# Diagonal loaded by quarters, layer 2's first mask in free tiles, bias of layer 2 behind the last norm

## The chip, the cores and the metric

The kernel runs on one core of one Trainium2 chip. The metric is device time in microseconds (us) of one execution; the median of three runs is given. The profile is of one further execution, recorded by the hardware profiler. The engines are PE (matrix products), DVE (vector), ACT (scalar), POOL (GpSimd) and SP, which here only issues transfers (DMAs). Each engine works through its own list of instructions in order.

## What is computed

`x` has the shape (8, 2048, 64): batch, nodes, channels. `adj` is a 2048 × 2048 matrix whose nonzero elements in a row are all the same number, 1/degree, and whose diagonal is nonzero. Four layers run one after the other, each adding its result to `x` and normalizing over the channels:

```python
x = _layernorm(x + L0(x, adj, embedding, weight, bias))   # weights made per node from an embedding
x = _layernorm(x + L1(x, H, adj, W, W_ind, ...))          # attention over 64 hyperedges, and adj @ (x @ W_ind)
x = _layernorm(x + L2(x, adj, weight_self, weight_neighbor, bias))
x = _layernorm(x + L3(x, adj, W))                         # adj + I, scaled by degree on both sides

# L0: the terms x, adj x and 2 adj (adj x) - x, each times a per-node weight
As = [jnp.eye(N)]; As.append(A)
for _ in range(2, K): As.append(2.0 * (A @ As[-1]) - As[-2])

# L2
out_self = jnp.einsum('bni,io->bno', x, weight_self)
x_neighbors = jnp.einsum('nm,bmi->bni', adj, x)
out_neighbors = jnp.einsum('bni,io->bno', x_neighbors, weight_neighbor)
return out_self + out_neighbors + bias
```

## The kernel before, in words

`x` is held as 2048 rows of 512 numbers (8 batches × 64 channels), in 16 tiles of 128 rows. A product with `adj` is made with a mask of zeros and ones, which is exact in the fast matmul format, and the row's number is multiplied in afterwards. That number is the diagonal of `adj`: the column buffer `s1` holds it, 128 partitions × 16, one column for each tile of rows; `s2` is twice that (L499). The other factor of a product is split in two parts of that format, `hi` and `lo`, and both are multiplied. A mask of 128 columns and 2048 rows is 1 MB.

The stages, in the order of the profile:

- **First product** (0 to 148 us), `first_product`: y1 = adj x. There are 4 quarters `q` of 4 row tiles, and in each 8 pieces `n` of adjacency (512 KB), with 16 matmuls of about 0.229 us each. The call `begin(n + 2)` ahead of piece n's products has SP load the piece and DVE turn it into a mask (L447), so DVE stands two pieces ahead. In quarter 0 each `begin` also loads a piece of `x` (512 KB, xraw) and splits it into x_hi (ACT, L425) and x_lo (DVE, L426); x and adjacency share a pool of four raw buffers. At the end of a quarter ACT and DVE write y_hi and y_lo of its tiles with the scale `s1`. Between the matmuls stand steps of `prepare`, which makes lists out of H for layer 1: small PE products (sm, L381 and L399), DVE operations (pT_raw, L366, and its neighbours) and some transfers.
- **Layer 0** (148 to 718 us), `layer0`: it loads adjacency again by row tile (adj, L958), x (xT, L969; xs, L973), the embedding (et, L971), and the row `s_row` spread to all partitions (srow, L964), all on SP. DVE makes masks (L978), and SP stores them in DRAM (L979) for the later layers. POOL and DVE compare mask × `s_row` with the adjacency itself, and so check that its rows have the form that the kernel uses. The first loads are issued while the first product still runs.
- **Layer 1** (718 to 1072 us), `layer1`: its order is written out by hand as a list of turns under `program_order`, which makes the scheduler keep the order of the source. The layer's norm is in steps: the variance on DVE, epsilon and the power −1/2 on POOL (L829, L831), the scale on ACT (x2, L835). When the turns reach the last tiles, `layer2_steps` is advanced beside them: `features2` transposes a tile of the new x, and `layer2(j)` multiplies it by layer 2's two weights (u, L858), writes y_hi on ACT and y_lo on DVE, adds the self term to x2 on DVE (L867) and the bias to x2 on POOL (L871). `for _ in last: pass` finishes the steps that are left after the turns.
- **Layer 2** (1072 to about 1210 us): for each of 16 row tiles, a mask is loaded (L1394), multiplied with y_hi and y_lo (32 matmuls, L1399), and DVE adds `s1` × product to x2 (L1508). `mask_tile` takes the mask's buffer from a pool of three, mj2, opened after layer 1; its space was that of layer 1's buffers, so the first load waits for layer 1's last readers.
- **Layer 3** (to the end).

Tiles of 256 KB named `b0_0` to `b0_15` make up a buffer that first holds x_hi. Later they are given to other uses one by one: layer 1 takes most of them for names of its own. `industry_early` loads layer 1's first mask in four parts into four of them.

The diagonal is loaded at piece n = 7 of the source, L451 to L461, by four DMAs that POOL issues, one for each quarter (2 KB: 128 × 4 single elements), and a fifth, also POOL's, writes `s1` to DRAM as the row `s_row` of 2048 numbers, one element at a time. Since nothing holds them back, they stand first on POOL's queue.

Of the kernel before, what the change touches and what calls it, by code (L numbers as in the profile page):

```python
# [18 lines left out]
P = 128  # L19
# [12 lines left out]
class Tiles:  # L32
# [6 lines left out]
    def __getitem__(self, key):  # L39
        p, t, c = key  # L40
        if self.per == 1:
            return self.tiles[t][p, c]
        k, lo = divmod(c.start, QW)
        return self.tiles[t * self.per + k][p, lo:lo + c.stop - c.start]


def r_(ap):
# [4 lines left out]
def kernel(  # L52
# [358 lines left out]
    def first_product(own, pre, rawp, mskp, y_hi, y_lo, prepare):  # L411

        x_hi, x_lo = buffer(own, 0, "x_hi"), buffer(own, 1, "x_lo")
        with tc.tile_pool(name="acc0", bufs=7, space=PSUM) as ps_acc, tc.tile_pool(
            name="sm0", bufs=1, space=PSUM
        ) as ps_s:
            def split_x(g, h):
                raw = rawp.tile([P, 2, QW], F32, tag="raw", name=f"xraw_{g}_{h}")
                lo = g * QW + h * 2 * P
                nc.sync.dma_start(  # L420
                    raw, xn[lo:lo + 2 * P, :].rearrange("(t p) c -> p t c", p=P)
                )
                for t in range(2):
                    j = 4 * g + 2 * h + t
                    nc.scalar.copy(r_(x_hi[:, j, :]), raw[:, t, :])  # L425
                    nc.vector.tensor_tensor(  # L426
                        r_(x_lo[:, j, :]), raw[:, t, :], x_hi[:, j, :], ALU.subtract
                    )

            steps = prepare(ps_s)  # L430
            pieces = [
                (q, i, kk, h)
                for q in range(NQ)
                for i, kk in enumerate([q] + [kk for kk in range(4) if kk != q])
                for h in range(2)
            ]
            m_of, accs = {}, {}

            def begin(n):

                if n >= len(pieces):
                    return
                q, i, kk, h = pieces[n]
                raw = rawp.tile([P, 2, QW], F32, tag="raw", name=f"raw_{q}_{kk}_{h}")
                nc.sync.dma_start(raw, at[q, kk][:, 2 * h:2 * h + 2, :])
                m = mskp.tile([P, 2, QW], F32, tag="m", name=f"m_{q}_{kk}_{h}")
                nc.vector.tensor_scalar(r_(m), raw, 0.0, None, op0=ALU.is_gt)  # L447
                m_of[n] = m
                if q == 0:
                    split_x(kk, h)  # L450
                if n == 7:  # L451

                    for qq in range(NQ):
                        d = at[qq, qq]
                        nc.gpsimd.dma_start(
                            cols_of["s1"][:, 4 * qq:4 * qq + 4],
                            bass.AP(d.tensor, d.offset, [[4 * QW + 1, P], [QW + P, 4]]),
                        )
                    nc.gpsimd.dma_start(
                        s_row.rearrange("o (t p) -> p (o t)", p=P), cols_of["s1"]  # L460
                    )  # L461

            with program_order():
                begin(0)
                begin(1)
                for n, (q, i, kk, h) in enumerate(pieces):
                    begin(n + 2)
                    if i + h == 0:
                        accs[q] = [
                            ps_acc.tile([P, BC], F32, tag="acc", name=f"y1p_{4 * q + jj}")  # L470
                            for jj in range(4)
                        ]
                    m = m_of.pop(n)
                    for t in range(2):
                        mt = 4 * kk + 2 * h + t
                        for jj in range(4):
                            for part in (x_hi, x_lo):
                                nc.tensor.matmul(  # L478
                                    accs[q][jj],
                                    r_(m[:, t, jj * P:(jj + 1) * P]),  # L480
                                    r_(part[:, mt, :]),
                                    start=i + h + t == 0 and part is x_hi,
                                    stop=i == 3 and h + t == 2 and part is x_lo,
                                )
                        if n > 8 or (n, t) == (6, 0):
                            for _ in range(1 + t):
                                next(steps, None)
                    if (i, h) == (3, 1):
                        for jj in range(4):
                            j = 4 * q + jj  # L490
                            s = cols_of["s1"][:, j:j + 1]
                            nc.scalar.activation(r_(y_hi[:, j, :]), accs[q][jj], AF.Copy, scale=s)
                            nc.vector.scalar_tensor_tensor(
                                r_(y_lo[:, j, :]), accs[q][jj], s, y_hi[:, j, :],
                                op0=ALU.mult, op1=ALU.subtract,
                            )
                for _ in steps:
                    pass
            nc.vector.tensor_scalar(cols_of["s2"], cols_of["s1"], 2.0, None, op0=ALU.mult)  # L499

    @with_exitstack
    def layer1(
# [345 lines left out]
        def layer2(j):  # L848

            xT = xT_of.pop(j)  # L850

            pool, tag = ((ps_g, "g"), (ps_fc, "fc"))[j % 2]
            mm = pool.tile([P, 2, BC], F32, tag=tag, name=f"u_{j}")
            mm = mm.rearrange("p h (r c) -> p h r c", r=NP)
            for pr in range(NP):
                for h in range(2):
                    rs = slice(h * 64, (h + 1) * 64)
                    nc.tensor.matmul(  # L858
                        mm[:, h, pr, :], xT[rs, pr * P:(pr + 1) * P], w2_sb[rs],
                        start=True, stop=True,  # L860
                    )

            def by_half(t):
                return t[:, j, :].rearrange("p (r h c) -> p h r c", h=2, c=C)

            nc.scalar.copy(r_(by_half(i_hi)), mm[:, :, :, 0:C])
            nc.vector.tensor_tensor(by_half(x2), mm[:, :, :, C:2 * C], by_half(x2), ALU.add)  # L867
            nc.vector.tensor_tensor(
                r_(by_half(i_lo)), mm[:, :, :, 0:C], by_half(i_hi), ALU.subtract
            )  # L870
            nc.gpsimd.tensor_tensor(  # L871
                b_view(x2[:, j, :]), b_view(x2[:, j, :]),
                bias2_sb.unsqueeze(1).to_broadcast([P, B, C]), ALU.add,
            )

# [35 lines left out]
        with program_order():  # L913
            run(unit, 0, first)
            run(unit, 0, second)
            run(unit, 1, first)
            for t in range(NT + 3):
                now = {"p": (product, t), "q": (product, t - 1), "u": (unit, t + 1), "v": (unit, t + 2),
                       "s": (unit, t), "m": (mixer, t - 1), "o": (mixer, t - 2),
                       "f": (mixer, t - 3)}  # L920
                for turn_ in turns.split():
                    who, what = turn_.split(".")
                    run(*now[who], what)
                    if t > NT and 0 <= now[who][1] < NT:
                        next(last, None)
            for _ in last:
                pass
        return x2


    def layer0(
# [288 lines left out]
        def industry_early():  # L1220


            parts = []
            for q, home in enumerate((4, 6, 13, 14)):
                m = own.tile([P, 4, P], F32, tag=f"b0_{home}", name=f"m0_{q}")
                nc.sync.dma_start(m, masks[0][:, 4 * q:4 * q + 4, :])
                parts.append(m)
            acc = ps_acc.tile([P, BC], F32, tag="acc", name="ind_0")

            def steps():  # L1230
                for mt in range(NT):
                    for part in (y_hi, y_lo):
                        nc.tensor.matmul(
                            acc, r_(parts[mt // 4][:, mt % 4, :]), r_(part[:, mt, :]),
                            start=mt == 0 and part is y_hi, stop=mt == NT - 1 and part is y_lo,
                        )
                    yield
# [101 lines left out]
    def short_program(top):  # L1339
# [71 lines left out]
        with tc.tile_pool(name="l0", bufs=1) as l0, tc.tile_pool(  # L1411
# [39 lines left out]
                nc.vector.tensor_scalar(flag, bad[:, 0:1], -1.0, 1.0, op0=ALU.mult, op1=ALU.add)  # L1451


        x2 = layer1(
            own, wts, fcw_sb, fcb_sb, av_sb, fcg_sb, vecs, rden, hgr, aggp, agg_st, h_sb, y_hi,
            y_lo, mask_tile, times_mask, w2_sb, bias2_sb, ps_acc, early,
        )
# [3 lines left out]
        with tc.tile_pool(name="mj2", bufs=3) as mjp, tc.tile_pool(  # L1461
# [38 lines left out]
                )  # L1500

            for j in range(NT):
                a = mask_tile(mjp, j, "l2")
                acc = ps_acc.tile([P, BC], F32, tag="acc", name=f"a2_{j}")
                for mt in range(NT):
                    times_mask(acc, a, y_hi, y_lo, mt)
# [624 lines left out]
```

## Time and profile before

| | |
|---|---|
| median of 3 runs | 1344.24 us (1344.21 to 1349.38) |
| the profiled execution | 1349.78 us, its span 1347.8 us |
| PE busy | 1275.1 us, 95% |
| DVE busy | 915.7 us, 68% |
| POOL busy | 483.8 us, 36% |
| ACT busy | 370.7 us, 28% |
| mean granted PE clock | 0.960 |

The profiled execution is 5.5 us above the median, and 2.0 us of it lie outside the span. Times of single instructions are of this execution. A line of a timeline gives the start in us, the length, the engine, the line of the source, the operation with output and input, the number of instructions, and in brackets how long the engine idled before and for whom. The chain of waits is followed back from the last instruction; its pieces are given in order of time.

The transfers concerned, from the table of DMA issues (name, queue, number, size of one, median us from issue to landing):

```profile
raw<-in_at SPq DMA_DIRECT2D x32, 512.0 KB, 5.5
xraw<-in_xn SPq DMA_DIRECT2D x8, 512.0 KB, 5.5
s<-in_at POOLq DMA_DIRECT2D x4, 2.0 KB, 6.3
s_row<-s POOLq DMA_DIRECT2D x1, 8.0 KB, 11.5
mj_l<-mask SPq DMA_DIRECT2D x47, 1024.0 KB, 4.9
```

POOL's queue at the start and around layer 1's last norm:

```profile
1.36 1.00 POOL L455 DMA_DIRECT2D s<-in_at  x1 [0.36 <-issue]
2.72 2.27 POOL L455 DMA_DIRECT2D s<-in_at  x3
...
1054.15 1.27 POOL L871 TENSOR_TENSOR x<-x,bias_sb 128x512 f32<-128x512 f32 x1 [0.21 <-DVE x L867]
1055.94 1.27 POOL L871 TENSOR_TENSOR x<-x,bias_sb 128x512 f32<-128x512 f32 x1 [0.52 <-DVE x L867]
1057.18 0.23 POOL L829 TENSOR_SCALAR var<-var 128x8 f32<-128x8 f32 x1
1057.50 1.67 POOL L831 TENSOR_TENSOR rstd<-var,mhalf 128x8 f32<-128x8 f32 x1
1059.13 1.26 POOL L871 TENSOR_TENSOR x<-x,bias_sb 128x512 f32<-128x512 f32 x1
```

The whole span in 40 slices of 33.7 us (PE's busy tenths and its granted clock):

```profile
PE   6999899999999999999997599999998799999997
PEclk9999899999999999999997599999998999999999
```

### The profile page before, as it was taken

Reading aid. Unit: us, or ns where it says so; the run is one execution under the profiler, and the core shown is the slowest. Engines: PE = TensorE matmul, PEld = TensorE weight load, DVE = VectorE, ACT = ScalarE, POOL = GpSimd, SP = SyncE. Lnnn points to the kernel's source line nnn. Section 1 sums busy time; section 2 is a strip of 40 time slices with the busy share of each in tenths; the row PEclk is TensorE's granted clock in tenths of the full one; section 3 lists DMA queues with packets and bytes.
Section 4 is the critical chain, followed back from the end, with each engine's and each line's share of the span. In section 5 each row is a group of like instructions: output and inputs, shape, how many; then the busy total and the mean of one; then the engine's idle time right before and its main releaser. Section 6 shows DMA issues by size and latency. Waiting matters only on the chain.

```text
span 1347.8 us, 19945 instructions
## 1 busy us (share of the span) xinstructions
PE 1275.1 (95%) x7708; PEld 1010.0 (75%) x7708; DVE 915.7 (68%) x1559; ACT 370.7 (28%) x853; POOL 483.8 (36%) x403
## 2 busy tenths in 40 slices
PE   6999899999999999999997599999998799999997
PEld 5777688888888888888885376666666588888885
DVE  3556378787877777777663669899984646655454
ACT  2100101111222222222212446666664511111111
POOL 2000354444444444444210667777772600000000
PEclk9999899999999999999997599999998999999999
DMA  8976632333333333331604022222220133333451
GB/s 219 269 215 182 197 112 89 104 105 104 105 104 105 105 105 105 105 105 55 256 23 152 24 75 77 91 95 94 79 78 1 49 140 125 125 120 139 171 188 72
DMA packets 100358, 157.21 MB, mean 117 GB/s; under 512 B 12832, under 2 KB 64416, under 8 KB 94112
## 3 DMA queue, kind: packets, MB, share of 16 engines
q1 hardware_dynamic: 97776, 151.65, 34.7%
q10 hardware_dynamic: 2304, 4.20, 0.8%
q8 instruction: 63, 1.03, 0.3%
q14 instruction: 39, 0.32, 0.1%
q0 software_dynamic: 176, 0.02, 0.1%
HBM read 118.08 MB, written 37.76 MB: 116 GB/s over the span
## 4 chain that ended last, share of the span: by engine, by line
PE 77%; DVE 14%; DMA 3%; ACT 2%; issue 1%; POOL 1%; SPq 0%; DVEq 0%; ACTq 0%; POOLq 0%
PE pp L1081 25%; PE a L1399 18%; PE y2p L1044 9%; PE y1p L478 7%; PE ind L1399 4%; DVE d L703 3%; PE df L802 2%; DMA xraw<-in_xn 2%; DVE gp L700 2%; DVE gate L654 2%; DVE ez L723 1%; PE try L154 1%; PE yp L1489 1%; DVE coef L658 1%; DVE th L798 1%
## 5 line engine op out<-in xcount | busy, mean ns | idle before, releaser
L1092 DVE SCALAR_TENSOR_TENSOR r<-pp,emb_sb,r 128x256 f32<-128x256 f32 x512 | 247.2, 483 | 114.9 <-PE pp L1081 101.1
L1081 PE MATMUL pp<-w_sb,xT 64*128 64x256 f32 x1024 | 160.4, 390 | 1.7 <-DVE r L1092 1.7
L1030 POOL TENSOR_TENSOR r<-xs,bn 128x256 f32<-128x256 f32 x32 | 22.7, 731 | 384.8 <-issue 245.3
L1081 PE MATMUL pp<-w_sb,y1T 64*128 64x256 f32 x1024 | 153.5, 376 | 0.0
L1081 PE MATMUL pp<-w_sb,y2T 64*128 64x256 f32 x1024 | 153.5, 376 | 0.0
L478 PE MATMUL y1p<-x_hi,m 128*128 128x512 f32 x256 | 105.9, 414 | 12.0 <-ACT x_hi L425 11.6
L1081 PEld LDWEIGHTS pp<-w_sb,xT 64*128 64x128 f32 x1024 | 94.4, 186 | 25.1 <-issue 14.9
L1081 PEld LDWEIGHTS pp<-w_sb,y1T 64*128 64x128 f32 x1024 | 99.7, 187 | 10.9
L1081 PEld LDWEIGHTS pp<-w_sb,y2T 64*128 64x128 f32 x1024 | 99.6, 187 | 11.0
L1399 PE MATMUL a<-y_hi,mj_l 128*128 128x512 f32 x256 | 102.9, 402 | 5.0 <-DMA mj_l<-mask 5.0
L1399 PE MATMUL ind<-y_hi,mj_l 128*128 128x512 f32 x240 | 104.8, 437 | 0.0
L1044 PE MATMUL y2p<-y_hi,msk 128*128 128x512 f32 x256 | 103.4, 404 | 0.0
L1399 PE MATMUL a<-y_lo,mj_l 128*128 128x512 f32 x256 | 102.7, 401 | 0.0
L478 PE MATMUL y1p<-x_lo,m 128*128 128x512 f32 x256 | 102.6, 401 | 0.0
L1044 PE MATMUL y2p<-y_lo,msk 128*128 128x512 f32 x256 | 101.5, 396 | 0.0
L1399 PE MATMUL a<-v_hi,mj_l 128*128 128x512 f32 x256 | 100.1, 392 | 0.0
L1399 PE MATMUL a<-v_lo,mj_l 128*128 128x512 f32 x256 | 100.0, 391 | 0.0
L1399 PE MATMUL ind<-y_lo,mj_l 128*128 128x512 f32 x240 | 96.7, 403 | 0.0
L725 POOL TENSOR_TENSOR ez<-ez,coef 128x1024 f32<-128x1024 f32 x32 | 69.9, 2184 | 71.3 <-DVE ez L723 69.0
L986 POOL TENSOR_TENSOR ms<-msk,srow 128x1024 f32<-128x1024 f32 x32 | 89.9, 2810 | 5.2 <-DVE ms L999 5.2
L478 PEld LDWEIGHTS y1p<-x_hi,m 128*128 128x128 f32 x256 | 49.3, 192 | 24.8 <-ACT x_hi L425 12.0
L978 DVE TENSOR_SCALAR msk<-adj 128x1024 fp32r<-128x1024 f32 x32 | 63.7, 2024 | 3.9 <-DMA adj<-in_at 3.8
(273 smaller groups left out, 2430.5 us busy)
## 6 DMA issues: line engine op xcount, KB each, us to landing
mj_l<-mask SPq DMA_DIRECT2D x47, 1024.0 KB, 4.9
raw<-in_at SPq DMA_DIRECT2D x32, 512.0 KB, 5.5
adj<-in_at SPq DMA_DIRECT2D x64, 256.0 KB, 3.6
mask<-msk SPq DMA_DIRECT2D x32, 512.0 KB, 4.4
xraw<-in_xn SPq DMA_DIRECT2D x8, 512.0 KB, 5.5
oh<-oh SPq DMA_DIRECT2D x32, 128.0 KB, 2.6
xT<-in_xt SPq DMA_DIRECT2D x16, 256.0 KB, 3.1
xs<-in_xn SPq DMA_DIRECT2D x16, 256.0 KB, 2.9
```

Source lines behind the costliest of these rows:

```text
L478: nc.tensor.matmul(accs[q][jj], r_(m[:, t, jj * P:(jj + 1) * P]), r_(part[:, mt, :]), start=i + h + t == 0 and part is x_hi, stop=i == 3 a ...
L654: nc.vector.tensor_tensor(t[:, 0:3, :], ex[:, 0:3, k, :], hgr[:, j, k, :].unsqueeze(1).to_broadcast([P, 3, B]), op,)
L700: nc.vector.tensor_tensor(by_b(gp[:, 0:n]), by_b(gp[:, 0:n]), per_b(rest, 2 * i, n), ALU.mult)
L703: nc.vector.tensor_tensor(d, d, gp, ALU.add)
L725: nc.gpsimd.tensor_tensor(by_b(ez), by_b(ez), per_b(coef, 2 * i, 2), ALU.mult)
L802: nc.tensor.matmul(df[:, b:b + 1], th[:, b % 2, (b // 2) * P:(b // 2 + 1) * P], av_sb, start=True, stop=True,)
L978: nc.vector.tensor_scalar(r_(m), raws[j][h], 0.0, None, op0=ALU.is_gt)
L986: nc.gpsimd.tensor_tensor(ms, m, srow[j].unsqueeze(1).to_broadcast([P, 8, P]), ALU.mult)
L1044: nc.tensor.matmul(acc, r_(msk[j, mt // 8][:, mt % 8, :]), r_(part[:, mt, :]), start=mt == 0 and part is y_hi, stop=mt == NT - 1 and part ...
L1081: nc.tensor.matmul(pp[:, h, pl, :], terms[j][name][rs, 2 * bq + pl], w_sb[rs, k, dq * 4 * C:(dq + 1) * 4 * C], start=k == 0, stop=k == K - 1,)
L1092: nc.vector.scalar_tensor_tensor(rb, ppv[:, :, dd, :], emb_sb[:, j, d:d + 1], rb, op0=ALU.mult, op1=ALU.add)
L1399: nc.tensor.matmul(acc, r_(a[:, mt, :]), r_(part[:, mt, :]), start=mt == 0 and part is hi, stop=mt == NT - 1 and part is lo,)
```

## The change

Three edits. First, each quarter's part of the diagonal is loaded at the fourth piece of that quarter: DVE clears the quarter's four columns of `s1`, and POOL's DMA, which overwrites them, has to wait for that. The write of `s_row` follows the last quarter's DMA, and so does `s2`, which reads all of `s1`. Second, layer 2's first mask is loaded in four parts into the tiles b0_11, b0_15, b0_0 and b0_1; layer 1 does not use the first two, and has the other two for products that end earlier. The class `Parts` makes the four tiles look like one mask, and `industry_early` uses the same helper for its own mask. Third, the sixteen additions of layer 2's bias move out of `layer2(j)` behind the loop that finishes layer 2's steps.

In the built programs, PE's and ACT's instructions keep their order. POOL has all of layer 1's variances and powers ahead of the sixteen bias additions, where before the last power stood behind eight of them. DVE has four memsets more, and its `s2` stands behind the fourth of them and the prod operations of L1378. SP issues three DMAs more: two of the four parts stand at the beginning of layer 1, two late in it, and the load of mask 1 stands where that of mask 0 was.

```diff
+class Parts:
+    def __init__(self, parts):
+        self.parts = parts
+
+    def __getitem__(self, key):
+        p, t, c = key
+        return self.parts[t // 4][p, t % 4, c]
...
@@ first_product, begin(n)
-                if n == 7:
-
-                    for qq in range(NQ):
-                        d = at[qq, qq]
+                if n % 8 == 4:
+
+                    s1 = cols_of["s1"][:, 4 * q:4 * q + 4]
+                    nc.vector.memset(s1, 0.0)
+                    d = at[q, q]
+                    nc.gpsimd.dma_start(
+                        s1, bass.AP(d.tensor, d.offset, [[4 * QW + 1, P], [QW + P, 4]])
+                    )
+                    if q == NQ - 1:
                         nc.gpsimd.dma_start(
-                            cols_of["s1"][:, 4 * qq:4 * qq + 4],
-                            bass.AP(d.tensor, d.offset, [[4 * QW + 1, P], [QW + P, 4]]),
+                            s_row.rearrange("o (t p) -> p (o t)", p=P), cols_of["s1"]
                         )
-                    nc.gpsimd.dma_start(
-                        s_row.rearrange("o (t p) -> p (o t)", p=P), cols_of["s1"]
-                    )
...
@@ layer2(j)
-            nc.gpsimd.tensor_tensor(
-                b_view(x2[:, j, :]), b_view(x2[:, j, :]),
-                bias2_sb.unsqueeze(1).to_broadcast([P, B, C]), ALU.add,
-            )
...
@@ end of layer1
+            a_first = mask_parts(own, 0, (11, 15, 0, 1), "l2")
             for _ in last:
                 pass
-        return x2
+            for j in range(NT):
+                nc.gpsimd.tensor_tensor(
+                    b_view(x2[:, j, :]), b_view(x2[:, j, :]),
+                    bias2_sb.unsqueeze(1).to_broadcast([P, B, C]), ALU.add,
+                )
+        return x2, a_first
+
+    def mask_parts(own, j, homes, name):
+
+        parts = []
+        for q, home in enumerate(homes):
+            m = own.tile([P, 4, P], F32, tag=f"b0_{home}", name=f"mp_{name}_{q}")
+            nc.sync.dma_start(m, masks[j][:, 4 * q:4 * q + 4, :])
+            parts.append(m)
+        return Parts(parts)
...
@@ layer 2
             for j in range(NT):
-                a = mask_tile(mjp, j, "l2")
+                a = mask_tile(mjp, j, "l2") if j else a_first
```

More of the change, by code (lines that the diff above doesn't have):

```diff
@@ L1220, in industry_early @@
         def industry_early():
[L1223 to L1227, printed above, removed]
+            a = mask_parts(own, 0, (4, 6, 13, 14), "l1")
             acc = ps_acc.tile([P, BC], F32, tag="acc", name="ind_0")
@@ L1233, in steps @@
                         nc.tensor.matmul(
-                            acc, r_(parts[mt // 4][:, mt % 4, :]), r_(part[:, mt, :]),
+                            acc, r_(a[:, mt, :]), r_(part[:, mt, :]),
                             start=mt == 0 and part is y_hi, stop=mt == NT - 1 and part is y_lo,
@@ L1451, in short_program @@
                 nc.vector.tensor_scalar(flag, bad[:, 0:1], -1.0, 1.0, op0=ALU.mult, op1=ALU.add)
-        x2 = layer1(
+        x2, a_first = layer1(
             own, wts, fcw_sb, fcb_sb, av_sb, fcg_sb, vecs, rden, hgr, aggp, agg_st, h_sb, y_hi,
```

## The prediction

> **What bounds the kernel now.** I read the chain of waits first, then the 40 slices, then the three places where TensorE (PE) stops, by the windows and the timeline. The page gives the chain by engine:
>
> ```profile
> PE 77%; DVE 14%; DMA 3%; ACT 2%; issue 1%; POOL 1%; SPq 0%; DVEq 0%; ACTq 0%; POOLq 0%
> ```
>
> PE sets the pace, so only what stops PE can be won. The change touches two such stops. First the start, in the windows (stretch, length, busy us of PE, weight load, DVE, ACT, POOL, PE clock, DMA share, GB/s) and in the timeline:
>
> ```profile
> 12.00:14.00 2.00, 2.00 (x10) 1.65 (x9) 1.28 (x4) 0.72 (x2) 1.91 (x5) 1.00 1.12 316
> 14.00:16.00 2.00, 2.00 (x10) 1.65 (x9) 1.22 (x2) 0.42 (x1) 0.26 (x1) 1.00 1.43 77
> 16.00:18.00 2.00, 2.00 (x11) 1.63 (x10) 0.69 (x1) 0.00 (x0) 0.00 (x0) 1.00 0.69 43
> 20.00:22.00 2.00, 0.59 (x3) 0.16 (x1) 0.00 (x0) 0.00 (x0) 0.00 (x0) 1.00 0.53 50
> 26.00:28.00 2.00, 2.00 (x6) 1.52 (x6) 0.92 (x2) 0.00 (x0) 0.00 (x0) 0.50 1.05 412
> ```
> ```profile
> 10.68 1.17 POOL L459 DMA_DIRECT2D s_row<-s  x1 [5.44 <-DMA s<-in_at]
> 24.96 0.75 PE L478 MATMUL y1p<-x_hi,m 128*128 128x512 f32 x1 [4.37 <-ACT x_hi L425]
> ```
>
> Right after POOL issues the 8 KB write of s_row (10.68, landing 11.5 us later by the table of DMA issues), the transfers fall from 316 to some 43 to 77 GB/s, although the DMA engines count as busy. A 512 KB piece of x that normally takes 5.5 us takes 11.8, PE stands still from 20.42 to 24.96, and then runs at clock 0.50.
>
> Second, the passage from layer 1 to layer 2, in the chain of waits (start, us, what):
>
> ```profile
> 1055.94 1.27 POOL x L871
> 1057.21 0.22 POOL var L829
> 1057.50 1.68 POOL rstd L831
> ...
> 1061.74 1.24 PE u L858 x16
> ...
> 1071.53 1.18 PE u L858 x16
> ...
> 1072.85 4.71 DMA mj_l<-mask
> 1077.55 0.14 issue
> ```
> ```profile
> 1061.74 1.24 PE L858 MATMUL u<-w_sb,xT 64*128 64x128 f32 x16 [3.31 <-ACT xT L846]
> 1077.69 0.77 PE L1399 MATMUL a<-y_hi,mj_l 128*128 128x512 f32 x1 [5.00 <-DMA mj_l<-mask]
> ```
>
> A bias addition on POOL stands in front of the last norm's power, and PE has idled 3.31 us for that norm; then layer 2's first mask is only requested when layer 1's last u products are done, and PE idles 5.00.
>
> **What the Trainium skill says.** (1) "DMA: Bandwidth & Descriptors", section "Rules for kernel authors": a strided last dimension becomes one descriptor per element; its section "SWDGE vs HWDGE vs iDMA" has an engine change between queues only at a packet of up to 64 descriptors. s_row is written as 2048 single floats, so other queues wait behind such packets; the trace agrees (11.5 us for 8 KB, 43 to 77 GB/s beside it). (2) "TensorE: Matmul & The Clock Gate", section "What's actually happening": after some 3.4 us idle PE runs at half clock for about 3.4 us. The trace agrees: after 4.54 and 5.00 us idle the clock is 0.50. (3) "SBUF — State Buffer", section "SBUF: two separate sides": some DVE operations keep GpSimd from writing descriptors. No line of before shows it; it bears on how late the last diagonal DMA can land.
>
> **Part 1, the diagonal.** Removed from the start: four POOL issues at 1.36 to 4.98 and s_row's at 10.68. Gain: the hole, 24.96 − 20.42 = 4.54 us, and the slow clock after it (8 matmuls in 3.45 us instead of 8 × 0.229 = 1.83), 1.62; together 6.16. The pieces of adjacency and x share four buffers, and between 24 and 46 us the DMA share is 0.97, so some of it may come back as later waits: I take 5.5 (4 to 6.2). From 46 to 148 us PE is bound by itself (2.9 us of waits in all), so the gain lasts to the end of the product.
>
> Added: in each quarter a memset on DVE (0.06 us) and a DMA on POOL, idle there. The first three quarters cost nothing: their columns are read a dozen microseconds or more later, against a landing of 6.3. The fourth decides. Its memset stands where DVE is at 124.16 in before's time, POOL issues then, and it lands at about 130.4 (6.3 later; 130.0 to 131 by the four issues seen). Two things wait for it. *s2* = 2·s1 (L499), which ran at 13.01, now stands in DVE's order about where before has 127.0, so DVE waits 3.4 us. Queued behind it is the pT_raw operation (L366) that ran at 127.29; PE's sm product (L381) at 129.24 needs it, and PE needs the masks behind it: PE stops about 130.2 − 128.2 = 2.0 us (0 if it lands by 128.2, 2.8 if at 131; should DVE keep GpSimd from writing the descriptors, each us that it is later costs one more). And *s_row's write* now starts at 130.4 and, at its old 11.5, lands near 142. Its slow stretch began 3 us after issue, so from about 133.5 to 142 the engines move some 65 GB/s instead of the 178 that the window 130 to 142 has: (178 − 65) × 8.2 us = 0.93 MB late, at 285 GB/s 3.3 us. In that stretch layer 0's first adj, xT and xs loads are issued (137.44 to 147.58). DVE's mask of layer 0 (L978) already waits 1.88 us for adj at 146.60, and the first product's y_lo stands behind it; the first bp product at 152.83 waits for a DMA. So 3.3 us of late loads come through, and PE's 2.0 us stall lies beside them, not on top. With a little for the restart I take 3.5 lost (0 to 6). SP's srow load (L964, 148.38 in before) must wait for the write: 6.4 us of slack, nothing. Net of part 1: +2.0 (−2 to +6.2).
>
> **Part 2, layer 2's first mask.** The mask comes in four DMAs of 256 KB into tiles that were free or last used by layer 1's industry products, done by about 1000 in the trace. Two are issued at the start of layer 1, two late in it; SP issues three DMAs more, about 0.4 us each, where the DMA share is low (675 to 715 has none): nothing. The first product then waits only for y_hi and y_lo of tile 14 (PSUM), ready about 1073.1 instead of 1077.69: 4.6. It also keeps the clock: 13 matmuls start every 0.427 us instead of 0.227, 2.6. Sum 7.2 (5.5 to 7.5). Next late is mask 1, issued where mask 0 was (1072.85), landing in 4.7 at 1077.6; it is needed after 32 matmuls × 0.229 at 1080.4. Mask 2 follows at 1082 at the latest, needed at 1087.7.
>
> **Part 3, the bias.** The last variance is ready at 1055.26, but POOL is in L871; the power ends at 1059.17. Without it, 1055.26 + 0.22 + 0.1 + 1.68 = 1057.3: 1.85 gained. PE's idle time falls from 3.3 to 1.5 us, so the half clock until 1066 (u products 2.08 instead of 1.16, transposes 1.11 instead of 0.66; 1.4 lost) probably goes; I count 0.85 of it. Sum 2.7 (1.8 to 3.3). The sixteen additions (16 × 1.27 = 20.3 us, POOL 1057.3 to about 1078) lie beside PE; the first reader is layer 2's residual on DVE at 1080.4. If that cover went, tile 0 alone, 1.3 us, would matter.
>
> **Sum.** 2.0 + 7.2 + 2.7 = 11.9. The profiled execution took 1349.78 (span 1347.8 and 2.0 around it), so 1337.9; it is 5.5 over the median 1344.24, so on the median 1332.3: **1332**.
>
> **The rivals.** *(a) The hole at the start is not s_row's.* x and adjacency are both requested heavily there (316 GB/s before it), so a queue backlog could make it. For: landings of 13 us occur in that crowd. Against: 43 GB/s is no full queue. Then part 1 loses 2 to 3.5 and wins nothing: 1344.2 − 9.9 + 2.5 ≈ 1337. *(b) The moved write gives back all it saved.* Loads late by the whole 11.5 us stretch cost 5.5 to 7: part 1 ≈ −0.5, 1335. For: layer 0's start is DMA bound (285 GB/s, share 0.97). Against: the write partly precedes those loads. *(c) PE at layer 2's start waits for something else*, such as a part issued late on SP's queue behind another load: gain there 2 instead of 7.2, 1337.5 to 1339. *(d) Slower:* s_row's write lands so late that SP, in order, stands at the srow load and holds all layer 0 loads behind it. This must cost more than 5.5 + 7.2 + 2.7 = 15.4 us beyond before, so the write must take 11.5 + 6.4 + 15.4 ≈ 33 us, three times the measured one. With the layer 0 loads competing that isn't excluded: 1347 or more.
>
> **How the numbers follow.** Chances: forecast 0.55, (a) 0.10, (b) 0.18, (c) 0.12, (d) 0.05. The forecast's own range is 1328 to 1336 by the ends above; to hold (b), (a) and the near side of (c) it is 1326 to 1339. A change of 0.5%, 6.7 us, is about what a measurement of this kernel can tell from none; that bound is 1337.5. The forecast and (b) lie below it, (a) for the larger half, (c) mostly above: faster 0.83, same 0.12, slower 0.05.
>
> **What would show it.** Right: near 300 GB/s at 14 to 24 us and PE without a gap there; DVE idle about 3 us before s2, waiting for s; s_row landing around 135 to 137 in the new time, with a dip in GB/s before it; the power of the last norm 2 us after its variance, and the bias block behind it; layer 2's first matmul less than 1 us after the last u, at clock 1.00. Wrong: a hole at 20 us without s_row; PE at layer 2's start waiting for mask parts; or an SP stall at the srow load.

## The result, and the profile after

The changed kernel takes 1337.98 us (median of 7 runs, 1333.23 to 1338.65), the kernel before 1344.58 us in the same comparison (7 runs). The ratio is 0.9934, with a 95% interval of 0.9912 to 0.9956: 8.9 us faster (5.9 to 11.8), where 11.9 were forecast. The ratio is not the quotient of the two medians, which lie 6.6 us apart; it and its interval are used throughout, since the time of the kernel before differs between sets of runs (medians of 1344.58 to 1349.40). The profiled execution took 1338.11 us, its span 1336.3.

The start, in the windows of the changed kernel (columns as in the prediction):

```profile
14.00:16.00 2.00, 2.00 (x10) 1.65 (x9) 1.81 (x3) 0.68 (x2) 0.00 (x0) 1.00 0.98 371
16.00:18.00 2.00, 2.00 (x10) 1.66 (x9) 1.17 (x3) 1.14 (x2) 0.00 (x0) 1.00 0.67 218
20.00:22.00 2.00, 2.00 (x11) 1.63 (x10) 1.80 (x4) 0.69 (x2) 0.17 (x1) 1.00 0.99 378
26.00:28.00 2.00, 2.00 (x11) 1.63 (x10) 1.88 (x3) 0.47 (x1) 0.00 (x0) 1.00 0.99 356
```

The hole is gone: PE is full, the clock is 1.00, and where 43 to 77 GB/s moved, 218 to 378 do. But the same picture is now at the end of the first product. These are later windows of the same kernel:

```profile
122.00:124.00 2.00, 1.93 (x9) 1.50 (x9) 1.97 (x4) 0.00 (x0) 0.97 (x1) 1.00 0.29 17
126.00:128.00 2.00, 2.00 (x9) 1.37 (x9) 1.01 (x5) 0.00 (x0) 0.00 (x0) 1.00 1.64 14
128.00:130.00 2.00, 2.00 (x11) 1.65 (x10) 0.96 (x3) 0.00 (x0) 0.00 (x0) 1.00 0.70 10
130.00:132.00 2.00, 2.00 (x10) 1.38 (x9) 0.80 (x4) 0.00 (x0) 0.00 (x0) 1.00 1.05 15
136.00:138.00 2.00, 0.00 (x0) 0.00 (x0) 0.00 (x0) 0.00 (x0) 0.00 (x0) 0.98 0.33 76
138.00:140.00 2.00, 0.00 (x0) 0.00 (x0) 0.00 (x0) 0.00 (x0) 0.00 (x0) 0.50 0.96 279
```

A DMA share of 1.05 or 1.64 with 14 or 15 GB/s is not a busy transfer. A share above 1 can only come about if packets count for as long as they are outstanding, so these transfers had all but stopped. The timelines of four engines, in order of time, show what this does:

```profile
117.27 0.75 POOL L467 DMA_DIRECT2D s<-in_at  x1 [34.54 <-DVE s L465]
121.24 0.17 DVE L511 TENSOR_SCALAR s<-s 128x16 f32<-128x16 f32 x1 [0.59 <-DMA s<-in_at]
121.79 1.18 POOL L471 DMA_DIRECT2D s_row<-s  x1 [3.77 <-DMA s<-in_at]
127.34 5.97 SPq L1389 DMA_DIRECT2D w_sb<-in_w2s  x1
136.07 2.62 SPq L981 DMA_DIRECT2D adj<-in_at  x4
140.49 0.69 DVE L1001 TENSOR_SCALAR msk<-adj 128x1024 fp32r<-128x1024 f32 x1 [8.12 <-DMA adj<-in_at]
141.56 0.42 PE L392 MATMUL sm<-tri,pT 64*128 64x64 f32 x1 [5.69 <-DVE oh L415]
```

Read it from above. The last diagonal lands 3.9 us after its issue, and DVE waits 0.59 us. POOL issues s_row's write at 121.79 (this trace has no record of its landing; in e2 below it took 12.7 us). SP then needs 5.97 us for one issue (0.62 us for the same one before), and so comes to layer 0's first adj load at 136.07. That is to the hundredth when before came to it, although everything had run 7 us earlier. DVE has layer 0's mask ahead of its small operation oh, stands 8.12 us for adj, and PE stands 5.69 us for oh.

The passage to layer 2, from the chain of waits and PE's timeline of the changed kernel:

```profile
1051.99 0.25 POOL var L841
1052.31 1.68 POOL rstd L843
```
```profile
1056.55 1.16 PE L870 MATMUL u<-w_sb,xT 64*128 64x128 f32 x16 [1.48 <-ACT xT L858]
1066.74 0.47 PE L1418 MATMUL a<-y_hi,mp_l 128*128 128x512 f32 x1 [0.52 <-DVE y_lo L880]
```

The power follows its variance at once, PE idles 1.48 us for the last norm instead of 3.31, and 0.52 us in front of layer 2's first product instead of 5.00. The clock stays at 1.00 from 1059 to 1070 us.

**Where the time went, instruction by instruction.** PE executes the same instructions in the same order in both kernels, so each PE instruction's start can be compared with its start in the profile of before. The table gives the median difference in us over the 10 us that follow each time (of the profile of before); a negative number is ahead of before. Part 1 lies between the start and 160 us, the passage from layer 0 to layer 1 between 690 and 740, part 3 between 1050 and 1070, part 2 between 1070 and 1080.

| kernel | 100 | 160 | 690 | 740 | 1050 | 1070 | 1080 | 1200 |
|---|---|---|---|---|---|---|---|---|
| changed | −7.1 | +0.3 | +0.3 | −3.9 | −3.4 | −6.5 | −13.5 | −12.7 |
| changed, again (e10) | −7.1 | +0.7 | +0.8 | −6.0 | −6.9 | −10.0 | −17.0 | −16.1 |
| e1 parts 2 and 3 | +2.3 | +3.3 | +3.3 | −3.1 | −4.5 | −7.6 | −14.7 | −14.2 |
| e2 part 1 | −6.2 | +1.2 | +1.2 | −5.6 | −2.8 | −2.7 | −1.9 | −2.0 |
| e3 row turned | −6.4 | −4.6 | −4.5 | −11.3 | −12.3 | −15.4 | −22.5 | −22.0 |
| e4 row by quarters | −0.5 | +9.8 | +9.8 | +4.5 | +3.4 | +0.2 | −6.8 | −6.0 |
| e5 early, turned | −7.3 | −7.2 | −7.2 | −13.8 | −15.0 | −18.1 | −25.2 | −24.7 |
| e5 again (e11) | −5.5 | −5.3 | −5.3 | −6.0 | −8.7 | −11.8 | −18.8 | −18.3 |
| e6 extra dense write | −5.7 | +1.5 | +1.5 | +1.8 | +1.4 | −1.7 | −8.7 | −8.2 |
| e7 extra spread write | −5.5 | −5.3 | −5.3 | −12.4 | −12.4 | −15.5 | −22.5 | −22.0 |
| e8 part 3 | +2.2 | +2.9 | +3.0 | +2.9 | −0.3 | −3.4 | −3.5 | −3.0 |
| e9 part 2 | +2.6 | +3.1 | +3.1 | +1.0 | −0.4 | −0.4 | −7.4 | −7.4 |

The changed kernel is 7.1 us ahead at 100 us and has given all of it back at 160. Part 3 then wins 3.1 us and part 2 7.0. The gains of up to 7 us around 740 belong to none of the parts, as will be seen.

### The profile page after: what moved, and what is told of

Read it like the earlier page. It is cut to its first block, busy times and chain, and to the rows that moved or that the text cites. A ratio compares the mean times of both kernels' runs of the same rounds, so it can differ in the third digit from the quotient of the medians.

```text
span 1336.3 us, 19966 instructions
## 1 busy us (share of the span) xinstructions
PE 1267.3 (95%) x7708; PEld 1004.3 (75%) x7708; DVE 916.1 (69%) x1563; ACT 370.7 (28%) x853; POOL 484.5 (36%) x403
## 4 chain that ended last, share of the span: by engine, by line
PE 78%; DVE 14%; issue 3%; DMA 2%; ACT 2%; POOL 1%; SPq 0%; DVEq 0%; ACTq 0%; POOLq 0%
PE pp L1104 25%; PE a L1418 17%; PE y2p L1067 9%; PE y1p L490 8%; PE ind L1418 4%; DVE d L715 2%; PE df L814 2%; DVE gp L712 2%; DVE gate L666 2%; DVE ez L735 1%; PE yp L1508 1%; PE try L165 1%; DMA oh<-oh 1%; DVE coef L670 1%; PE aggp L1224 1%
## 5 line engine op out<-in xcount | busy, mean ns | idle before, releaser
L1418 PE MATMUL a<-y_lo,mj_l 128*128 128x512 f32 x240 | 95.0, 396 | 0.0
L1418 PE MATMUL a<-y_hi,mj_l 128*128 128x512 f32 x240 | 95.0, 396 | 0.0
```

The lines of the kernel that those rows point to most:

```text
L1418: nc.tensor.matmul(acc, r_(a[:, mt, :]), r_(part[:, mt, :]), start=mt == 0 and part is hi, stop=mt == NT - 1 and part is lo,)
```

## The experiments

Theory A was that s_row's write stops the other transfers wherever it stands, so that part 1 only carried the stop from 14 us to 122 us. The first four kernels (e1 to e4) undo or isolate part 1 and alter the write.

**e1: part 1 undone.** The diagonal's block in `begin` is that of the kernel before.

```diff
-                if n % 8 == 4:
-                    ...
+                if n == 7:
+                    for qq in range(NQ):
+                        ...
```

> The changed kernel with the diagonal's loads and s_row's write back where they were (part 1 undone; the mask's parts and the moved bias stay). Theory A (part 1 only carries the stop of the transfers from 14 us to 122 us and gains nothing; all of the gain is that of parts 2 and 3): as fast as the changed kernel or faster, 1334 to 1338 us, with PE's hole at 20 to 25 us back and none at 135 to 141. Rival B (part 1 pays some 2 us as forecast, and parts 2 and 3 pay less than 9.9 because the work behind them takes it back): 2 us or more slower than the changed kernel, 1340 us.

Measured: 1336.36 us, ratio 0.9907 (0.9878 to 0.9936), at least as fast as the changed kernel's 0.9934. Most of the gain is that of parts 2 and 3, as theory A has it; the intervals overlap, so that a gain or loss of some 2 us by part 1 stays possible. The table adds one thing: with the write in its old place this execution is 2.3 us later at 100 us than the profile of before, as are e8 and e9. s_row landed after 13.9 us here, 14.3 in e8 and 14.6 in e9, against 11.5 in the profile of before, which was a mild case of its own hole: PE waits 5.97 us for x_hi here, 4.37 there.

**e2: part 1 alone.** The converse edit, on the kernel before.

> The kernel before with part 1 alone. Theory A: 1344 us within 1, the interval around no change; PE is some 7 us ahead at 50 to 120 us and level with before at 150 us. Rival B: 1342 us.

Measured: 1345.59 us, 0.9984 (0.9969 to 0.9999), 2.2 us faster (0.1 to 4.2). That is nearer to rival B's 2 us than to nothing. The trace has both halves of theory A, 6.2 us ahead at 100 and 1.2 behind at 160. Both fit together if the old hole is taken at its usual size. In the old place the shift at 690 us is 0, 3.3, 3.0 and 3.1 (before, e1, e8, e9), on the mean 2.4; in the new place 0.3, 0.8 and 1.2, on the mean 0.8. By these traces part 1 wins about 1.6 us net. The times leave its sign open: e2's interval just excludes zero, while e1, without part 1, has the lower ratio (0.9907 against 0.9934 and, in the repetition below, 0.9913, with overlapping intervals).

**e3: the same place, other elements.** DVE turns the 16 columns in 32 x 32 blocks, and the row is written in 64 runs of 128 B.

```diff
...
+                        nc.vector.memset(wide, 0.0)
+                        nc.vector.tensor_copy(wide[:, 0:NT], cols_of["s1"])
+                        nc.vector.transpose(turned, wide)
-                        nc.gpsimd.dma_start(
-                            s_row.rearrange("o (t p) -> p (o t)", p=P), cols_of["s1"]
-                        )
+                        for b in range(4):
+                            nc.gpsimd.dma_start(
+                                s_row.rearrange("o (t b c) -> b t (o c)", b=4, c=32)[b],
+                                turned[32 * b:32 * b + NT, :],
+                            )
```

> The changed kernel, but DVE turns the 16 columns in blocks of 32 x 32, and POOL writes s_row in four DMAs of 16 runs of 128 B (64 runs where it wrote 2048 single floats), at the same place. Theory A (the single elements of the write stop the other transfers, and with them SP, which stands 6 us in one issue): the transfers of 122 to 134 us don't stop, SP doesn't stand, PE has no hole of 5.7 us, and the time falls by up to 7 us against the changed kernel, to about 1332. Rival C (SP's own run of small loads and stores, or the order on DVE with layer 0's mask ahead, bounds this stretch whatever the write does): the hole stays for the most part, 1337 us or more.

Measured: 1329.43 us, 0.9860 (0.9830 to 0.9890), faster than both kernels. SP's issues there take 2.09 us at most, and PE has no wait of 5.69. Rival C falls. What is left of the loss is another wait, the longest of PE's waits in this kernel between 7 and 140 us after the first load (who waits, for whom, us in total, times, longest) and in its windows:

```profile
PE pf L372 <- DVE pT L368: 1.6, 1, 1.6
```
```profile
120.00:122.00 2.00, 0.40 (x2) 0.00 (x0) 1.46 (x8) 0.00 (x0) 0.13 (x1) 1.00 0.23 35
122.00:124.00 2.00, 1.97 (x5) 1.47 (x6) 1.43 (x3) 0.00 (x0) 1.85 (x4) 0.65 0.37 77
```

PE waits for pT (L368). In the changed kernel DVE makes pT at 116.89, ahead of the memset; here it stands behind the new copy and the turning:

```profile
118.87 0.47 DVE L1405 TENSOR_TENSOR prod<-wb,vecs 64x64 f32<-64x64 f32 x2 [1.09 <-DMA vecs<-in_a_node]
121.16 0.17 DVE L475 COPY wide<-s 128x16 f32<-128x16 f32 x1 [0.33 <-DMA s<-in_at]
121.50 0.39 DVE L368 TENSOR_SCALAR pT<-pT_raw 128x512 fp32r<-128x512 f32 x1
```

The copy itself waits only 0.33 us for the last diagonal load. Most of the delay is DVE's order: the prod operations of layer 1, with 1.09 us of waiting for a load of their own, also come ahead of pT. The 3.1 us that the expectation of e5 gives as DVE's wait is POOL's wait for the turned columns.

**e4: the row by quarters**, 512 floats behind each quarter's load.

```diff
-                    if q == NQ - 1:
-                        nc.gpsimd.dma_start(
-                            s_row.rearrange("o (t p) -> p (o t)", p=P), cols_of["s1"]
-                        )
+                    nc.gpsimd.dma_start(
+                        s_row[:, 4 * q * P:4 * (q + 1) * P].rearrange("o (t p) -> p (o t)", p=P), s1
+                    )
```

> The changed kernel with s_row written by quarters, each 512 single floats behind its own quarter's load. Theory A: the stop is proportional to the elements, 11.5 / 4 = about 3 us each; the first three fall where the loads are two pieces ahead, the last costs 2 to 3 us of the 7: about 1334 us. Rival C: the hole stays, 1337 us or more. Rival D (a fixed cost for each write): more stops in quarters 1 to 3, and slower than the changed kernel.

Measured: 1345.98 us, 0.9985 (0.9965 to 1.0004). Theory A's proportion fails and the outcome is rival D's: each quarter's write takes as long to land as the whole did. Lines of this kernel's table of DMA issues, and of its windows behind the first write (28.46 us):

```profile
s_row<-s POOLq DMA_DIRECT2D x4, 2.0 KB, 11.6
```
```profile
28.00:32.00 4.00, 4.00 (x20) 3.26 (x19) 1.30 (x3) 1.14 (x2) 2.19 (x6) 1.00 0.98 244
32.00:36.00 4.00, 4.00 (x19) 3.30 (x18) 1.35 (x5) 0.00 (x0) 0.00 (x0) 1.00 1.12 91
36.00:40.00 4.00, 4.00 (x19) 3.08 (x17) 0.00 (x0) 2.42 (x4) 0.00 (x0) 1.00 0.71 59
40.00:44.00 4.00, 0.17 (x1) 0.00 (x0) 1.17 (x2) 0.00 (x0) 0.00 (x0) 0.80 0.91 252
```

512 floats land after 11.0 to 13.1 us, as 2048 do. In the differences to the profile of before, the first write costs 6.0 us of the lead, the third 3.1 and the last 7.2. Only the second falls into slack.

So it was not the number of elements. The next kernels ask what else it could be: the fifth takes the diagonal's wait and pT's delay away, and the sixth and seventh add a write that nobody reads or waits for.

**e5: the last two quarters' diagonals loaded together**, at the fourth piece of the third quarter; the turning stays where e3 has it.

```diff
-                    s1 = cols_of["s1"][:, 4 * q:4 * q + 4]
-                    ...
+                    for qq in ((q,) if q < 2 else (2, 3) if q == 2 else ()):
+                        s1 = cols_of["s1"][:, 4 * qq:4 * qq + 4]
+                        ...
```

> The third experiment's kernel with the last quarter's diagonal loaded one quarter earlier, beside the third's, so that DVE's turning of the columns, at the fourth piece of the last quarter, finds it there. Theory A (what was left of the loss in the third experiment is DVE's wait of 3.1 us for the last diagonal load, which held PE 2.1 us and half its clock): no gap of PE at 120 to 122 us and 2 to 4 us less than the third experiment, about 1326 on its scale, 0.983 to 0.985 of the kernel before. Rival C (layer 0's first loads bound it anyway): no faster than the third, 0.986.

Measured: 1331.84 us, 0.9882 (0.9861 to 0.9904), no faster than e3 in time, and outside the 0.983 to 0.985 of theory A. The same kernel ran again as e11, in a later set of runs:

> The fifth experiment's kernel once more. Theory A: faster than the changed kernel by 5 to 9 us, 0.984 to 0.990 of the kernel before, and PE without a gap between 6 and 140 us.

1327.28 us, 0.9835 (0.9813 to 0.9857). In e5's trace PE's longest wait between 7 and 140 us, the first load apart, is 0.4 us, and the lead at 160 is 7.2 us instead of e3's 4.6. In e11's it is 5.3, with one wait of 0.9. So e3's gap is gone, but e3 and e5, which ran on different chips, cannot be told apart by their times. Beside e11, the changed kernel ran once more:

> The changed kernel once more, on the same chip as the next one. Theory A: 0.991 to 0.996 of the kernel before; the gap of PE at 135 to 141 us is there again, and the passage from layer 0 to layer 1 is short or long as the clock's windows fall.

1335.54 us, 0.9913 (0.9886 to 0.9941), with PE's gap again (5.82 us, ended at 141.73). In that set the fifth kernel is 8.3 us faster than the changed one by the medians, and the intervals do not meet.

**e6 and e7: an extra write, dense or spread**, behind e5's four.

```diff
+    spare = scr.tile([1, N], F32, tag="spare", name="spare")
...
+                        nc.gpsimd.dma_start(
+                            spare.rearrange("o (t p) -> p (o t)", p=P), cols_of["s1"]
+                        )
```

In e7 the spare row has 16 N floats (16 x 2048), and the target is `spare.rearrange("o (t p g) -> p (o t) g", p=P, g=16)[:, :, 0:1]`.

> The fifth experiment's kernel and, behind its four writes of s_row, one more write that nobody reads: the same 2048 single floats to a spare row of 8 KB, each beside the next, as the kernel before wrote s_row. Theory A: the transfers stop for 11 to 13 us, PE gets its hole back, 6 to 10 us slower than the fifth. Rival E (it was the wait for the row, by SP or by the order of the queues, and not the write itself): as fast as the fifth, since nobody waits for the spare row.

> As the sixth, but the 2048 single floats are spread, one in every 64 bytes of a spare row of 128 KB. Theory F (the cost is of many small writes to the same stretch of 64 bytes, each waiting for the one before, which is why 512 floats took as long as 2048): the write lands in 3 to 5 us and the kernel is within 1 or 2 us of the fifth. Rival G (the cost is of each single element, or a fixed one for such a write): it lands in 11 to 13 us and costs what the sixth costs.

e6 took 1340.45 us, 0.9934 (0.9913 to 0.9955); e7 took 1329.15, 0.9858 (0.9830 to 0.9886). The spare write in the table of DMA issues, and two windows, of e6:

```profile
spare<-s POOLq DMA_DIRECT2D x1, 8.0 KB, 12.4
```
```profile
124.00:126.00 2.00, 2.00 (x10) 1.64 (x10) 1.75 (x7) 0.00 (x0) 0.00 (x0) 1.00 0.06 1
138.00:140.00 2.00, 0.00 (x0) 0.00 (x0) 0.00 (x0) 0.00 (x0) 0.00 (x0) 0.84 0.97 276
```

The same of e7:

```profile
spare<-s POOLq DMA_DIRECT2D x1, 8.0 KB, 5.4
```
```profile
124.00:126.00 2.00, 2.00 (x10) 1.65 (x11) 1.41 (x5) 0.00 (x0) 0.00 (x0) 1.00 0.37 56
138.00:140.00 2.00, 2.00 (x11) 1.65 (x10) 0.50 (x3) 0.00 (x0) 0.00 (x0) 1.00 1.00 318
```

Nobody waits for the spare row, and still the dense write costs 8.6 us against e5: rival E falls, the write itself does it. The spread one, with as many elements of the same size from the same queue, costs nothing that shows, and rival G falls too. POOL's queue carried 304 packets in both traces, so the number of packets isn't it either. Where the elements land decides. Theory F had expected the spread write to land in 3 to 5 us; it took 5.4.

**e8 and e9: parts 3 and 2 alone**, by the edits of the change's diff.

> The kernel before with the bias moved and nothing else. Up to 1040 us its instructions are those of the kernel before, so that its trace also shows how far two executions of them lie apart. Theory A (the trace's shift of 3.1 us at 1060 is part 3's own): layer 1's last rstd 2 us after its variance, u 3 us earlier, layer 2's first mask as late behind u as before, about 3 us faster in all. Rival H (the passage from layer 0 to layer 1, 4 to 6 us shorter in every run so far than in the profile of before, was shortened by part 1 or part 2): here that passage is as long as in the profile of before. If it is short here too, it is chance of the one execution.

> The kernel before with part 2 alone (the first mask of layer 2 in four parts; the diagonal and the bias as before). Theory A (parts 2 and 3 add up): layer 2's first product starts less than 1 us behind y_lo of tile 14 instead of 5 us behind the last u, 7 us gained there in the trace and about 6 left at 1200 us; 0.993 to 0.997. Rival I (part 2 pays only where part 3 has moved the bias out of the way): 3 us or less.

e8: 1342.21 us, 0.9964 (0.9949 to 0.9979), 4.8 us faster (2.8 to 6.9), 3.1 of it in the trace at 1060. e9: 1338.64, 0.9917 (0.9891 to 0.9943); the trace has 7.0 us at layer 2's start, without part 3's help, and rival I falls. e9's time gains more than that, 11.2 us (7.7 to 14.7, four runs), and misses the 0.993 to 0.997 expected. The times of e2, e8 and e9 add up to 18.2 us, where the whole change gained 8.9 and 11.7: single times are too coarse to size a part. They go with the mean clock of the run (the kernel before beside e9 took 1344.57 us at 0.965 and 1352.14 at 0.959). That this makes up e9's surplus is likely, and not shown.

In e8 the passage around 700 to 740 us is as long as in the profile of before. That looked like rival H, but e6, which has parts 1 and 2, is as long, and e2, e1 and e5 are all short. e5 and e11 are one and the same kernel, and between 690 and 740 e5 gains 6.6 us on the profile of before and e11 0.7. What goes with it is the granted clock. The windows 705 to 712 of before, e8, e6, e11 (long), and of e1, e7 and e5 (short), each from its own trace:

```profile
705.00:712.00 7.00, 5.92 (x38) 4.51 (x39) 1.66 (x5) 1.80 (x5) 1.60 (x2) 0.74 0.11 40
```
```profile
705.00:712.00 7.00, 7.00 (x34) 5.45 (x34) 1.72 (x5) 0.94 (x2) 1.68 (x1) 0.59 0.10 39
```
```profile
705.00:712.00 7.00, 5.92 (x31) 4.23 (x30) 1.68 (x5) 1.56 (x3) 2.26 (x2) 0.69 0.21 75
```
```profile
705.00:712.00 7.00, 6.97 (x32) 5.35 (x33) 1.53 (x6) 1.53 (x5) 1.66 (x2) 0.57 0.42 139
```
```profile
705.00:712.00 7.00, 5.71 (x44) 4.43 (x43) 2.78 (x6) 2.31 (x4) 2.73 (x2) 1.00 0.23 76
```
```profile
705.00:712.00 7.00, 5.79 (x25) 3.85 (x24) 3.64 (x12) 1.30 (x3) 1.04 (x1) 1.00 0.79 258
```
```profile
705.00:712.00 7.00, 5.55 (x24) 3.16 (x24) 3.62 (x10) 1.31 (x2) 0.01 (x1) 1.00 0.81 277
```

The PE clock here, the third number from the end of each line, is 0.57 to 0.74 in the long ones and 1.00 in the short ones. The shift does not order them: +3.3 (e1) and −5.3 (e7) are short, +3.0 (e8) and −5.3 (e11) long. The Trainium skill ("TensorE: Matmul & The Clock Gate", section "What's actually happening") says that the activity window of this clock runs freely, so that the same kernel measures differently from run to run. The runs agree: layer 1's start leaves PE partly idle, and whether the clock drops there is not the change's doing. It goes with 5.9 us between the two executions of one kernel, e5 and e11.

## Why the prediction was right

**Direction, size, range.** 11.9 us forecast, 8.9 measured (5.9 to 11.8), and 11.7 us (8 to 15) in the repetition, 0.9913 of 1349.40 us. As a time, 1337.98 lies 6 us above the 1332 named: inside the stated 1326 to 1339, outside the forecast's own 1328 to 1336, and where rivals (a) and (c) had put it (1337; 1337.5 to 1339). It is the traces, not the time, that speak against these two. That own range was narrower than its parts: their ends add up to 5.3 and 17.0 us, which is 1327 to 1339. By its steps it was right in two parts and right only by cancelling errors in the third, and that is luck.

**Part 2** (7.2 forecast): 7.0 or 7.1 in every trace that has it. It comes of the two terms named: the first product starts 0.52 us behind the last u instead of 5.00, and there is no half clock. The parts were there long before, and mask 1 came in time.

**Part 3** (2.7 forecast): 3.1 or 3.2 in every trace that has it. The half clock goes entirely, where I counted 0.85 of 1.4 us. "The sixteen additions lie beside PE" was nearly right: the traces with part 3 give back 0.5 to 0.9 us of it over layer 2's first tiles (−13.5 at 1080, −12.7 at 1200; e9, without it, has −7.4 at both). What holds PE up there I did not try to find.

**Part 1** (+2.0 net forecast): about 1.6 by the traces and 2.2 (0.1 to 4.2) by e2's time, but its terms were wrong.
- *The gain at the start*, 5.5 taken, is 7.1 against the profile of before and about 8.6 against the mean of the four traces with the old hole (mean shift at 100 us +1.8, of the three with the new place −6.8). The reserve for the four buffers was not needed, and the one profiled execution had a small hole.
- *PE's 2.0 us for s2* did not come. The last diagonal landed 3.9 us after its issue, not 6.3 as four loads at the crowded start had, and DVE waited 0.59 us; nothing shows of DVE keeping POOL from issuing it. e3 has a relative of this stall, 1.6 us of PE's waiting behind an operation that needs the diagonal, but there DVE's order made most of it, so the step as predicted is not shown anywhere.
- *The write's cost*, 3.5 taken, is 7.4 in the changed kernel (−7.1 to +0.3). Here the step failed that counted 0.93 MB of late loads at 285 GB/s. The bytes came late, and more than that: SP stood in an issue for 5.97 us, and behind it stood every load of layer 0; the loads that I priced were thus requested late and had not begun. The order on DVE then brought adj's landing to PE within the first product. Rival (b), the write gives back all it saved, was therefore right about the profiled execution, and the price that I gave it (5.5 to 7) was the better one; measured against the usual hole, some 1.6 us stay.
- *Why the write stops the others.* The prediction had other queues wait behind packets of single elements. e7 has as many single elements and packets as e6 and doesn't stop the transfers, so that step is wrong or incomplete. The spacing of the targets decides; why it does stays open.

Rivals (a), (c) and (d) fall: no transfers stop at 14 us without the write, PE does not wait at layer 2's start, and SP passes the srow load at 149.21 us without a stall. Of the 11.7 us between the two profiled executions, about 3.7 (+0.3 at 690, −3.4 at 1050) go with the clock around layer 1 and not with the change. The sum of the parts in the traces, 1.6 + 7.0 + 3.1 − 0.7 = 11.0, lies within the intervals of both times of the whole change; e9's own time is above its part, as said.

## What to carry to other kernels

Before a small transfer is moved out of a critical place, ask why it is expensive: moved, it took its stop of the other transfers along here, and what helped was its form (64 runs in place of 2048 floats took it from 12 us or more to 4). A lead that the trace shows at one point is worth nothing until the next fixed point has been looked at; comparing the starts of the same instructions in two traces shows in one table where each part is won and lost. One profiled execution is one draw: a hole or a clock window read from it may be some microseconds from the usual.

## What the runs showed of the hardware

- A DMA of single floats to neighbouring addresses of DRAM took 11.0 to 14.6 us whether it had 2048 or 512 of them, and the core's other transfers slowed meanwhile, in stretches nearly to a stop (1 to 91 GB/s in the windows shown). With the same 2048 floats set 64 B apart it took 5.4 us, and 64 runs of 128 B in four DMAs landed after 3.1 to 3.9 us each. The Trainium skill ("DMA: Bandwidth & Descriptors", section "Specifications") says that below 512 B the DMA engine reads, modifies and writes; no run here shows that directly. Many such for the same stretch of memory, one behind the other, would explain why the number doesn't count and the spacing does. Only the two spacings were tried, so this reading is supported and not shown.
- While such a write was outstanding, SP's issue of an ordinary load took 5.97 us instead of 0.62 (5.71 in e10; six issues of oh took 8.46 us in e6 instead of 3.87 in e7): the stop reached the issuing engine, and with it everything in its queue.
- Where PE is partly idle, the half clock came or stayed away from one execution to the next; between e5 and e11, the same kernel, 5.9 us go with it.
